# Own rows of a tile gathered four turns ahead instead of five, and the norm of its query three turns ahead instead of four, in a two-layer graph kernel

## The chip, the cores and the metric

The kernel runs on one core of one Trainium2 chip. The metric is device microseconds of one execution. The engines are named as the profile names them: PE is TensorE (PEld its weight loads), DVE is VectorE, ACT is ScalarE, POOL is GpSimd and SP is SyncE. DVE, ACT, PE, POOL and SP each work through a queue of their own in order, and wait for each other with semaphores.

## The reference

There are 4096 nodes with 512 features and an adjacency matrix with few edges: a random one of density 0.000976562, made symmetric, with the diagonal added. Two layers follow each other.

```python
h = jnp.maximum(_layernorm(x), 0.0)
Q, K, V = (h @ W.T for W in (WQ, WK, WV))          # 8 heads of 64
attn = softmax(Q K^T * 0.125 + (Q @ we.T + be), masked by adj)
hard = (attn == max(attn, axis=-1)) / 8            # the best neighbour alone
x = x + hard @ V
h = jnp.maximum(_layernorm(x), 0.0)
agg = (adj > 0) @ h / degree
out = concat(h @ W_self + b_self, agg @ W_nb + b_nb) @ W_comb + b_comb
x = x + relu(out)
```

In the first layer every node takes, for each head, the value row of the one neighbour with the highest score. In the second it takes the mean of its neighbours.

## The kernel before, in words

`sparse_path` does the work (`general_path` follows only for inputs with longer neighbour lists, and did not run). It has three stages.

The first stage (up to about 300 us) normalises all rows, projects keys and values, packs the adjacency matrix into lists of neighbours, sorts the nodes by their number of neighbours, and leaves all of it in a table `K_d` in device memory: a row holds a node's values, keys, list of neighbours with some numbers, and its own x.

The middle stage (about 300 to 905 us) is the one that the change touches. The sorted nodes are cut into 32 tiles of 128 rows. `CAPS` (L512) gives the longest list of each tile, from 24 down to 5. Each tile is worked on in one **turn**; the list `turns` (L1571 to L1573) says which tile comes in which turn, and "place p" below is the tile of turn p. The order is 0, 1, 24, 2, 25, 3, 26, 14, 4, 27, 5, 15, 6, 16, 7, 17 and so on: tiles with long lists ("apart", 0 to 13) and with short ones ("fused", 14 to 31) alternate for most of the stage.

A tile passes through these steps, each written to one or two engines' queues:

- `rows` (L1162): POOL gathers the tile's own rows from `K_d`, by `perm`. They land in one of 8 buffers `km` (1088 numbers a row), or, for the fused tiles of places 15 to 27 ("wide"), in a slot of a large tile `room` (1600 numbers a row). The buffer is read until the addition `xo` (L1318) several turns later, and a new gather into it has to wait for that.
- `query_norm` (L1175): ACT copies the list into `sidx` (L1177) and the row's numbers into `smeta` (L1180), and normalises the row into `hq` (L1182; 2 buffers).
- `query_turn` (L1187): PE transposes `hq` (L1156). `query_copy` (L1190): ACT copies the result into `hqT` (L1193). `query` (L1195): PE projects it into `q` (L636), eight matmuls as the profile counts them.
- `key_gathers` (L1200): POOL gathers the neighbours' rows, one gather of 128 rows for each place in the list. An apart tile's keys go to the 4 buffers `kg`, four neighbours in each. A fused tile's keys and values go together to a region of `room`.
- `scores` (L1238): DVE multiplies with `q` (L1244) and sums by head (L1250), four neighbours at a time.
- `winners` (L1266): DVE finds the best neighbour of each head. A fused tile takes its value at once by predicated copies (L1290) into `o`. An apart tile computes an index (L1312), and POOL gathers the 8 heads' values two or three turns later (`value_gathers`, L1221).
- `own_values` (L1229): POOL gathers a fused tile's own value rows into `o` where they did not come with `rows`.
- `layer1_xo` (L1315): DVE adds x and `o` (L1318). `layer1_stats`, `layer1_norm`, `layer1_turn`, `layer1` and their companions take the tile through the second layer's norm and projections and write it to `G_d` and `X1_d`.

POOL's gathers are all recorded at one line, L1121, in `gather`. The stage is written under a manual schedule: the order of the calls in the loop at L1652 is the order in each engine's queue. The loop runs from -5, so the first tiles' own rows and norms come ahead of turn 0. Within a turn POOL's order is: key gathers, mixed with the value gathers that are due, then `rows`, then `own_values`. ACT's order within a turn has `query_copy`, `layer1_copy`, `layer1_stats`, `query_norm`, `layer1_out`, `layer1_norm` and `ranks` (copies of neighbours' indices, L1264), besides the making of one-hot words (`hot_some`) for the last stage. On PE the product of those words (`hot_product`) comes before the scores of the turn, and `query_turn` at the end of it.

Turn 3 also ends with `fold_bias` (L1471): DVE work on a bias row, with casts (L1478) and subtractions (L1480). Nine value tiles are still projected and written in turns 0 and 1 (L847), and the first fused tile's gathers need them.

In the last stage (905 us to the end) POOL gathers rows of `G_d` for the sums over neighbours, DVE adds them up (L1830), PE does the eight tiles with the longest lists as a dense product (L1805), and the rows go out.

Of the kernel before, what the change touches and what calls it, by code (L numbers as in the profile page):

```python
# [544 lines left out]
def sparse_path(  # L545
# [70 lines left out]
    def load_fold(k):  # L616
        nc.sync.dma_start(
            F[:, ds(2 * k * NC, NC), :],
            (wselfT, wnbT)[k].rearrange("(c p) f -> p c f", p=P),
        )  # L620
        nc.sync.dma_start(
            F[:, ds((2 * k + 1) * NC, NC), :],
            wcomb[ts(k, D), :].rearrange("(c p) f -> p c f", p=P),
        )
# [13 lines left out]
    with ExitStack() as pa:  # L638
# [198 lines left out]
        def values(t, ps):  # L837
            pv = ps.tile([P, D], F32, tag="pm", name="pv")
            project(pv, hT(t), ws["wv"])
            return pv  # L840

        def values_out(t, pv, pool, eng, vs=None):
            if vs is None:
                vs = pool.tile([P, D], F32, tag="gs", name="vs")

            nc.scalar.activation(vs, pv, AF.Copy, scale=1.0 / H)
            return eng.dma_start(K_d[ts(t, P), 0:D], vs)  # L847
# [90 lines left out]
        def on(step, t, *args):  # L938
            if 0 <= t < KT:
                step(t, *args)  # L940
# [170 lines left out]
    with ExitStack() as pb:  # L1111
# [8 lines left out]
        def gather(dst, src, idx, at=0):  # L1120
            last[0] = nc.gpsimd.indirect_dma_start(  # L1121
                out=dst, out_offset=None, in_=src,
                in_offset=bass.IndirectOffsetOnAxis(ap=idx, axis=0), element_offset=at,
            )
            if at:

                beyond.append(last[0])
                for w in written:
                    tc.declare_no_dep(last[0].ins, w.ins, reason="other columns")
# [99 lines left out]
        def own_values(r):  # L1229

            s = st[r]
            if r in wide:
                s["o"] = s["own"][:, 0:D]
            else:
                s["o"] = xp.tile([P, D], F32, tag="o", name="o", bufs=3)
                gather(s["o"], K_d[:, :], perm[:, r : r + 1])
# [22 lines left out]
        def ranks(r, a=None, b=None):  # L1259

            if a is None and r == turns[0]:
                a = 4
            for kk, g0, g in st[r]["kg"][1:][a:b]:
                nc.scalar.copy(sidx[:, ds(sat[r] + g0, g)], kk[:, :, D])  # L1264
# [178 lines left out]
        def load_bias():  # L1443
            for k in range(2):
                fb = bp.tile([P, D], F32, tag=("own", "gs")[k], name="fb", bufs=1)
                for c in range(NC):
                    nc.vector.tensor_copy(
                        fb[:, ts(c, P)], bcs[k][:, c : c + 1].to_broadcast([P, P])
                    )
                fbs.append(fb)  # L1450
# [54 lines left out]
        def hot_some(i):  # L1505

            for _ in range(HOTS // 2):
                if i < FIRST or not hots or pos[hots[0][0]] >= i:
                    break
                if hot_now and hot_now[-1][0] != hots[0][0]:  # L1510
                    break
                r, k = hots.pop(0)
                if k == 0:
                    word_codes(r)
                code = st[r]["code"]
                one = bp.tile([P, SEG], BF16, tag="hot", name="hot", bufs=HOTS)
                nc.scalar.activation(one, ramp, AF.Square, bias=code[:, 0, k : k + 1])  # L1517
                nc.scalar.activation(one, one, AF.Relu, bias=code[:, 1, k : k + 1], scale=-1.0)
                hot_now.append((r, k, one))
# [14 lines left out]
        def words_copy():  # L1534
            for r, k, acc in summed:
                st[r]["wg"] = bp.tile([P, SEG], F32, tag="wst", name="wg", bufs=1)
                nc.scalar.copy(st[r]["wg"], acc)

        def words_turn():

            for r, k, acc in summed:
                if k < CAPS[r] - 2:
                    continue
                pt = pst.tile([P, NC, P], F32, tag="tr", name="tr")
                for h in range(2):
                    nc.tensor.transpose(pt[:, h, :], st[r]["wg"][:, ts(h, P)], ident)
                wi = bp.tile([P, 2, P], I32, tag="wst", name="wi", bufs=1)
                nc.scalar.copy(wi, pt[:, 0:2, :])
                nc.sync.dma_start(W_d[r], wi)
            summed.clear()  # L1550
# [51 lines left out]
        i = 0  # L1602
# [20 lines left out]
        def late(step, kind, i, *args):  # L1623

            out_ = []
            for r in turns:
                if plan[kind].get(r) == i:
                    out_ += step(r, *args) or []
            return out_

        def tail_turn(r):

            k = tail.index(r)
            at = HALF_R + TAIL0 + k * D
            st[r]["hT1"] = room[:, at : at + D].rearrange("p (c q) -> p c q", q=P)
            nc.scalar.copy(st[r]["hT1"], st[r]["hnp"])
# [15 lines left out]
        for i in range(-5, KT):  # L1652


            if i == -3:
                load_fold(0)
            if i == 0:
                load_bias()
                nc.gpsimd.memset(rows3, 0.0)
                for k in range(3):  # L1660
                    nc.gpsimd.memset(rows3[k * Q32 : k * Q32 + 1, :], 1.0)
            if i == KT - 1:
                wT = wp.tile([P, DENSE, SEG + 2], I32, tag="w_a", name="wT")
                nc.sync.dma_start(
                    wT[:, :, 0:SEG], W_d.rearrange("r p h q -> p r (h q)")
                )
            if i == 2:
                wS = wp.tile([P, NC, D], F32, tag="w_b", name="swS")
            if i == 1:
                wN = bp.tile([P, NC, D], F32, tag="swN", name="swN", bufs=1)  # L1670
            a, b = on(key_gathers, i), late(value_gathers, "value", i)
            while a or b:
                for q, n in ((a, max(1, round(len(a) / max(1, len(b))))), (b, 1)):
                    for g in q[:n]:
                        gather(*g)
                    del q[:n]
            on(rows, i + 5)
            if i in (0, 1):
                n = 6 if i == 0 else len(late_v)
                for k, t in enumerate(late_v[:n]):  # L1680
                    vs = xp.tile([P, D], F32, tag="xo", name="vs", bufs=2)
                    w = values_out(t, values(t, psm), None, nc.sync, vs)
                    for g in beyond:
                        tc.declare_no_dep(w.ins, g.ins, reason="other columns")
                    written.append(w)
                    if k < 4 and i == 0:
                        ranks(turns[0], k, k + 1)
                del late_v[:n]
            words_copy()
            late(layer1_move, "move", i)  # L1690
            on(query_copy, i + 2)
            late(layer1_copy, "layer1", i)
            early = [r for r in tail if plan["turn"][r] == i - 1]
            for r in early:
                tail_turn(r)
            if i >= 0 and turns[i] in fused:
                own_values(turns[i])
            on(query, i + 1)
            late(layer1_close, "move", i)
            words_turn()  # L1700
            hot_some(i)
            late(layer1_stats, "stats", i)
            on(query_norm, i + 4)
            late(layer1_out, "move", i)
            hot_some(i)
            for part in between.get(i, ()):
                fold(*part)
            late(layer1, "layer1", i)
            for r in early[: -1 if i == KT - 1 else None]:
                tail_product(r)  # L1710
            hot_product()

            def within():
                late(layer1_inverse, "stats", i)

            if i >= 0:
                scores(turns[i], within)
            if i == KT - 2:
                gsl = [gp.tile([P, GRP, D], F32, tag="kg", name="gs") for _ in range(2)]
            on(winners, i)  # L1720
            late(layer1_norm, "stats", i)
            if i == max(between):
                fold_bias()
            on(ranks, i)
            on(query_turn, i + 3)
            if i < KT - 1:
                late(layer1_turn, "turn", i)
                for r in early:
                    tail_move(r)
# [209 lines left out]
```

## Time and profile before

| | |
|---|---|
| median of 3 runs (lowest to highest) | 1190.85 us (1189.97 to 1191.04) |
| the profiled execution's own time | 1188.29 us |
| its span, first to last instruction | 1186.5 us |
| mean granted TensorE clock | 0.928 |
| moved by DMAs | 348.44 MB, mean 294 GB/s |
| own-rows gathers into `km` (L1121) | 25, of 0.94 us on POOL; 4.4, 5.5 and 9.8 us (least, median, most) to landing |
| norms of a query (L1182) | 32, of 0.81 us on ACT |

The page gives for each engine its busy time, its share of the span and its instructions. A group's line has the source line, the engine, the operation, the tile written and those read. In the views of waits, "A <- B" means that A stood idle and that B ended the wait. In the view by time a bracket holds the idle time before an instruction and what ended it; "issue" is time in which nothing that the profile shows was waited for. A view of windows gives each engine's busy time between two moments. All moments are microseconds from the start of the span.

### The profile page before, as it was taken

How to read it: one execution, taken by the hardware profiler on the slowest of the kernel's cores; microseconds unless marked ns; L12 is line 12 of the kernel's file. 1: busy time of each engine (PE TensorE's matmuls, PEld its weight loads, DVE VectorE, ACT ScalarE, POOL GpSimd, SP SyncE). 2: the span in 40 equal slices, each digit the busy share in tenths (PEclk: the TensorE clock that was granted, in tenths of full speed). 3: DMA queues.
4: the chain of work that ended last, by engine and by line, in shares of the span. 5: the costliest groups of instructions: out<-in, count | busy, mean ns of one | idle time of the engine just before them, and what ended most of it. 6: DMA issues, size and time to landing. Idle time of an engine off the chain costs nothing. (4 is left out here: it accounts for less than half of the span.)

```text
span 1186.5 us, 11454 instructions
## 1 busy us (share of the span) xinstructions
PE 1023.9 (86%) x3079; PEld 501.6 (42%) x3079; DVE 982.7 (83%) x1548; ACT 550.1 (46%) x1222; POOL 715.1 (60%) x939
## 2 busy tenths in 40 slices
PE   3999999979599668688879989888989999999792
PEld 1555555644244224344334434444434444444340
DVE  4358789889289798798989999999983699998894
ACT  3777777932222377486567678754462100000000
POOL 3332323312677757757777777777713777777774
PEclk9999999989799878889889889888999999999996
DMA  9999999979797678889898889988865888888973
GB/s 353 418 420 418 413 418 375 396 226 293 229 269 251 180 233 261 255 278 292 281 289 281 284 280 298 291 279 280 284 256 171 306 310 275 321 288 276 369 242 108
DMA packets 115594, 348.44 MB, mean 294 GB/s; under 512 B 21472, under 2 KB 23552, under 8 KB 107328
## 3 DMA queue, kind: packets, MB, share of 16 engines
q0 software_dynamic: 60560, 201.01, 53.0%
q1 hardware_dynamic: 50560, 146.56, 32.5%
q10 hardware_dynamic: 4400, 0.05, 0.3%
q8 instruction: 26, 0.43, 0.1%
q14 instruction: 48, 0.39, 0.1%
HBM read 287.75 MB, written 64.00 MB: 296 GB/s over the span
## 5 line engine op out<-in xcount | busy, mean ns | idle before, releaser
L1805 PE MATMUL da<-gk,mk 128*128 128x512 f32 x512 | 223.2, 599 | 6.9 <-DVE mk L1556 6.2
L1121 POOL DMA_INDIRECT room<-G_d,sidx x174 | 168.5, 969 | 84.6 <-issue 80.7
L636 PE MATMUL q<-wq,hqT 128*128 128x512 f32 x256 | 151.0, 745 | 51.3 <-DVE pr L1244 51.3
L1250 DVE TENSOR_REDUCE sc<-pr 128x32 f32<-128x2048 f32 (+3 forms) x114 | 183.3, 1608 | 3.8
L1121 POOL DMA_INDIRECT kg<-K_d,sidx x161 | 153.4, 953 | 49.0 <-issue 40.2
L1830 DVE TENSOR_REDUCE acc<-room 128x512 f32<-128x4096 f32 (+5 forms) x23 | 153.0, 6651 | 32.5 <-DMA room<-G_d,sidx 30.6
L1805 PEld LDWEIGHTS da<-gk,mk 128*128 128x128 f32 x512 | 98.2, 192 | 131.9 <-issue 123.1
L1121 POOL DMA_INDIRECT room<-K_d,sidx x118 | 111.6, 945 | 42.9 <-issue 25.6
L1121 POOL DMA_INDIRECT o<-K_d,vi x112 | 108.1, 965 | 34.2 <-issue 32.0
L636 PE MATMUL pk<-wk,room 128*128 128x512 f32 x256 | 118.5, 606 | 2.6 <-ACT room L821 2.6
L636 PE MATMUL pv<-wv,room 128*128 128x512 f32 x256 | 112.6, 592 | 0.0
L636 PEld LDWEIGHTS q<-wq,hqT 128*128 128x128 f32 x256 | 59.2, 243 | 123.0 <-issue 77.7
L1244 DVE TENSOR_TENSOR pr<-q,kg 128x2048 f32<-128x2048 f32 (+3 forms) x47 | 93.3, 1985 | 11.2 <-DMA kg<-K_d,sidx 10.1
L1393 PE MATMUL pr<-swS,hT 128*128 128x512 f32 x216 | 97.1, 592 | 0.0
L636 PE MATMUL pg<-swN,hT 128*128 128x512 f32 x216 | 97.1, 593 | 0.0
L760 ACT ACTIVATE mkt<-adjt,sgb 128x2048 bf16<-128x2048 int32 x44 | 88.0, 1999 | 2.1 <-POOL adjt L678 2.1
L1244 DVE TENSOR_TENSOR pr<-q,room 128x2048 f32<-128x2048 f32 (+3 forms) x42 | 73.2, 1744 | 18.1 <-DMA room<-K_d,sidx 16.0
L636 PEld LDWEIGHTS pv<-wv,room 128*128 128x128 f32 x256 | 48.3, 190 | 59.3 <-issue 59.1
L636 PEld LDWEIGHTS pk<-wk,room 128*128 128x128 f32 x256 | 47.5, 196 | 51.5 <-issue 47.8
L830 DVE SCALAR_TENSOR_TENSOR ks<-pk,swe 128x512 f32<-128x512 f32 x32 | 21.9, 686 | 52.5 <-PE pk L636 46.8
L1517 ACT ACTIVATE hot<-ramp,code 128x256 bf16<-128x256 bf16 x105 | 52.5, 500 | 22.5 <-DVE code L1498 22.5
L779 PE MATMUL pw<-mkt,planes 128*128 128x256 bf16 x512 | 62.8, 277 | 0.0
(254 smaller groups left out, 1619.5 us busy)
## 6 DMA issues: line engine op xcount, KB each, us to landing
adjt<-adj_dram SPq DMA_DIRECT2D x44, 1024.0 KB, 10.4
room<-adj_dram SPq DMA_DIRECT2D x20, 1024.0 KB, 11.0
x<-X_d SPq DMA_DIRECT2D x25, 512.0 KB, 7.8
xt<-x_dram SPq DMA_DIRECT2D x32, 256.0 KB, 8.1
K_d<-ks POOLq DMA_DIRECT2D x32, 256.0 KB, 6.5
X_d<-xo SPq DMA_DIRECT2D x32, 256.0 KB, 4.5
G_d<-gs SPq DMA_DIRECT2D x32, 256.0 KB, 3.9
gk<-G_d SPq DMA_DIRECT2D x16, 512.0 KB, 4.8
```

Source lines behind the costliest of these rows:

```text
L636: nc.tensor.matmul(dst, h[:, c, :], w[:, c, :], start=(c == 0), stop=(c == NC - 1))
L760: nc.scalar.activation(mk, st[t]["adj"][j], AF.Sigmoid, bias=sgb, scale=400.0, accum_out=degs[:, t, j : j + 1],)
L779: nc.tensor.matmul(pw, planes[:, s, :], st[t]["mk"][j][:, ts(i, SEG)], start=False, stop=(s == NPL - 1),)
L830: nc.vector.scalar_tensor_tensor(ks.rearrange("p (h d) -> p h d", h=H), st[t]["pk"].rearrange("p (h d) -> p h d", h=H), HD**-0.5, web.unsq ...
L1121: last[0] = nc.gpsimd.indirect_dma_start(out=dst, out_offset=None, in_=src, in_offset=bass.IndirectOffsetOnAxis(ap=idx, axis=0), element_o ...
L1244: nc.vector.tensor_tensor(pr[:, :g, :], s["q"].unsqueeze(1).to_broadcast([P, g, D]), kk[:, :, 0:D], ALU.mult)
L1250: nc.vector.tensor_reduce(sc[:, g0 : g0 + g, :], pr[:, :g, :].rearrange("p g (h d) -> p g h d", h=H), AX.X, ALU.add,)
L1393: nc.tensor.matmul(pr, s["hT1"][:, c, :], wS[:, c, :], start=False, stop=(c == NC - 1 and mine is None and not open_))
L1517: nc.scalar.activation(one, ramp, AF.Square, bias=code[:, 0, k : k + 1])
L1805: nc.tensor.matmul(dacc[r], masks[s][:, r, h, :], keys[s][:, h, :], start=(s == 0 and h == 0), stop=(s == NPL - 1 and h == 1),)
L1830: nc.vector.tensor_reduce(acc, g[:, 0:n, :].rearrange("p n f -> p f n"), AX.X, ALU.add)
```

## The change

The own rows of a tile are asked for four turns before its own turn, not five, and the norm of its query is asked for three turns before, not four. The transposes, the copy and the projection of the query keep their turns (three, two and one before).

```diff
@@ -1674,7 +1674,7 @@
                     for g in q[:n]:
                         gather(*g)
                     del q[:n]
-            on(rows, i + 5)
+            on(rows, i + 4)
             if i in (0, 1):
                 n = 6 if i == 0 else len(late_v)
...
@@ -1700,7 +1700,7 @@
             words_turn()
             hot_some(i)
             late(layer1_stats, "stats", i)
-            on(query_norm, i + 4)
+            on(query_norm, i + 3)
             late(layer1_out, "move", i)
             hot_some(i)
```

`on(step, i)` calls a step for the tile of place i where there is one. In both kernels one turn lies between a tile's `rows` and its `query_norm`.

## The prediction

> **What bounds the kernel now.** I read the page first, then a table of windows over the middle stage (312 to 905 us, where both edits lie), then what DVE and POOL waited for in it, and last the two engines in order of time around the longest waits. The page's first part, for the whole span:
>
> ```profile
> PE 1023.9 (86%) x3079; PEld 501.6 (42%) x3079; DVE 982.7 (83%) x1548; ACT 550.1 (46%) x1222; POOL 715.1 (60%) x939
> ```
>
> POOL's 60% misleads, as the windows show (columns: length; busy time and instructions of PE, weight loads, DVE, ACT, POOL; clock; DMA share; GB/s):
>
> ```profile
> 312.00:416.50 104.50, 93.32 (x227) 42.68 (x228) 83.34 (x78) 27.85 (x73) 79.19 (x86) 0.91 0.80 240
> 416.50:423.30 6.80, 1.10 (x4) 0.30 (x3) 6.39 (x16) 1.24 (x3) 0.03 (x1) 0.91 0.57 227
> 423.30:507.90 84.60, 63.56 (x178) 31.19 (x177) 72.72 (x85) 58.75 (x155) 64.44 (x67) 0.82 0.83 254
> 507.90:516.00 8.10, 5.93 (x13) 2.95 (x12) 7.79 (x13) 6.47 (x18) 0.00 (x0) 0.50 0.77 307
> 516.00:700.00 184.00, 154.71 (x427) 74.21 (x426) 170.44 (x208) 127.00 (x338) 139.47 (x147) 0.88 0.89 283
> 700.00:860.00 160.00, 144.97 (x406) 69.02 (x405) 153.42 (x197) 99.66 (x273) 121.29 (x128) 0.94 0.90 284
> ```
>
> From 516 to 700, 147 gathers in 184.0 us are 1.25 us each; 700 to 860 gives 160/128 = 1.25 again. A gather is busy 0.94 us and followed by 0.30 us of issue: POOL issues without a break, though it counts as 76% busy. Only the second and fourth rows hold nothing on POOL. DVE is 93 to 96% busy from 516 on. So two engines run neck and neck: DVE computes, POOL feeds it. What DVE, then POOL, waited for from 312 to 905 (total us, times, longest):
>
> ```profile
> DVE pr L1244 <- DMA room<-K_d,sidx: 16.0, 7, 5.1
> DVE pr L1244 <- DMA kg<-K_d,sidx: 10.1, 5, 3.3
> DVE o L1290 <- DMA o<-K_d,perm: 2.2, 1, 2.2
> ```
> ```profile
> POOL km L1121 <- DVE xo L1318: 14.9, 2, 8.1
> POOL room L1121 <- ACT sidx L1264: 7.2, 1, 7.2
> ```
>
> DVE waits for gathers that come late; POOL itself was held twice, by an own-rows gather waiting for a buffer. POOL in order of time (start, us, instruction, idle before and releaser), at each hold:
>
> ```profile
> 415.59 0.93 POOL L1121 DMA_INDIRECT room<-K_d,sidx  x1 [0.31 <-issue]
> 423.32 0.94 POOL L1121 DMA_INDIRECT km<-K_d,perm  x1 [6.80 <-DVE xo L1318]
> ...
> ```
> ```profile
> 506.94 0.94 POOL L1121 DMA_INDIRECT room<-K_d,sidx  x1 [0.30 <-issue]
> 516.02 0.94 POOL L1121 DMA_INDIRECT km<-K_d,perm  x1 [8.14 <-DVE xo L1318]
> ```
>
> DVE a turn and a half after the first hold:
>
> ```profile
> 466.98 4.58 DVE L1290 COPY_PREDICATED o<-best,room 128x512 f32<-128x512 int32 x6 [2.16 <-DMA o<-K_d,perm]
> ...
> 476.06 2.29 DVE L1244 TENSOR_TENSOR pr<-q,room 128x2048 f32<-128x2048 f32 x1 [2.60 <-DMA room<-K_d,sidx]
> ...
> 485.82 2.29 DVE L1244 TENSOR_TENSOR pr<-q,room 128x2048 f32<-128x2048 f32 x1 [5.09 <-DMA room<-K_d,sidx]
> ```
>
> These three waits (9.85 us) follow the first hold. After the second DVE waits 3.10 (turn 11, at 557.0), 3.31 (turn 13), 0.51 (15), 1.36 (17; the view blames its own reciprocal, but the gather landed at 667.29 and DVE went on at 667.37), 1.06 (27) and 0.35: 9.69 us.
>
> **The change, part by part.** No instruction is added or dropped: 32 own-rows gathers, 32 norms (three ACT instructions each), the same DMAs. SP's order is the same; PE's is the same but for names; DVE moves one small `half`. POOL's and ACT's orders move.
>
> *The two holds.* In the old order turn 4 asks for place 9 (tile 27), which takes the km buffer that the addition at 422.36 to 423.05, in turn 4 itself, frees. In the new one turn 4 asks for place 8, whose buffer the addition ending at 390.4 freed; place 9 comes in turn 5, behind 12 key gathers, long after 423. Turn 9 asked for place 14 and waited for the addition ending at 515.75, of turn 9; now it asks for place 13 and waits for that of turn 8, at 499.0, some 7 us before POOL wants it, while the wait on 515.75 moves behind turn 10's gathers. POOL thus gains 6.80 - 0.30 = 6.50 us and 8.14 - 0.30 = 7.84 us.
>
> *One gather less ahead.* Four own-rows gathers, not five, stand before the first key gather, so key gathers come one slot (1.25 us) earlier. Part is lost. ACT now copies the first turned query before the second norm: the copy waits for PE until 313.0, so the second norm ends near 314.75 instead of 313.66, and place 0's query starts about 1.0 us later. Its matmuls run 0.855 us apart until 318.9 and 0.43 us after, so 1.04/0.855 = 1.2 matmuls move into the fast part: 0.5 us later at the end. DVE's first product (320.80) has room: it then waits 4.2 us for gathers in turn 0. But the value writes behind it land at 360.56, and place 2's first gather needs them; the new order wants that gather at 360.60, 1.24 us sooner than 361.84. With writes 0.5 us later I keep 0.5 of the 1.25 (ends: -0.9, were PE slow for one more 3.4 us, to 1.25).
>
> PE's clock row gives 0.5 until 318.9 and 1.0 after it; throughout the trace it changes on a 3.41 us grid. The Trainium skill (TensorE: Matmul & The Clock Gate, What's actually happening) has a free-running window of 3413 ns, one busy window of which releases the clock. By that rule the release stays at 318.9, as the query fills the window before it; were two busy windows needed, the query would end 1.9 us later and the 0.5 kept would be -0.9.
>
> *POOL beside the bias fold.* In the first hold DVE runs the fold: six casts of 0.42 us, three subtractions of 0.68 us (L1478 and L1480, 416.5 to 421.9). Five gathers will now stand beside them; the trace shows none there. Nearest rows: gathers that start within DVE's xo addition take 1.30, 1.37 and 1.36 us (437.08, 454.92, 471.58) instead of 0.94. Ends: 0, and 4.5 us if POOL stops for all nine. I take three subtractions times 0.4 = 1.2 us.
>
> The Trainium skill (SBUF — State Buffer, Who interferes with whom) says that a DVE copy or cast in a two-port mode shuts GpSimd out for the whole instruction. By it the casts cost too, up to the 4.5 us; the sum would be 3.3 us less. No run here shows it yet.
>
> *The sum.* POOL's lead S is 0.5 up to turn 4, 0.5 + 6.5 - 1.2 = 5.8 from turn 5, and 5.8 + 7.84 = 13.6 from turn 10. DVE's gain G rises only where it waited for a gather, and never above S. Turn 3: 0.5. Turn 7: min(0.5 + 9.85, 5.8) = 5.8. Turn 11: 8.9; 13: 12.2; 15: 12.7; 17: min(14.1, 13.6) = 13.6. It stays there. From 867 the chain is DVE's (POOL waits 7.2 us for ACT's copies and then 31.9 us for the last G_d write), so the last stage moves as a whole.
>
> *Is POOL stopped elsewhere?* Other waits on DVE in its queue leave enough: gathers into a fused tile's region need the predicated copies of the fused tile two turns before, with 7.1 us to spare in turn 13, 4.9 in 15, 4.5 in 17, 2.4 in 21. POOL's growth over DVE (S less G) is then 4.7, 1.4, 0.9 and 0. Buffers of keys leave some 10 us or more.
>
> *The norm.* PE's transposes of place i+3 stand at the end of turn i; the norm now stands in that turn, at the slot where place i+4's stood. That slot ended 1.1 us before PE came in turn 0 and at least 3.0 us before in all later turns, so I cost it at nothing; without that cover PE would wait, but the query it holds up is needed a turn later. The four own rows asked one turn later still land a turn before their norm.
>
> Profiled execution: 1188.29 us (span 1186.5) less 13.6 = 1174.7. It lies 2.56 us under the median 1190.85, from which the forecast is **1177.2 us**.
>
> **The rivals.**
> *DMA takes it back.* From 516 the 16 engines are 0.89 to 0.90 busy. From 416.5 to 516.0 they did 6.8 x 0.57 + 84.6 x 0.83 + 8.1 x 0.77 = 80.3 us of work; at 0.89 this needs 90.2 instead of 99.5 us, 9.3 saved of 14.3. With the 0.5 and without the fold's 1.2 that is a gain of 9.8, 1181; were the engines full at 0.85 already, 80.3 / 0.85 = 94.5 us would leave 5.5, 1185. For it: that share. Against: POOL's cadence held at 0.90.
> *The fold takes 4.5 us,* POOL standing still beside all nine instructions: S ends 3.3 us lower, gain 10.3, 1180.5. For it: the stretched gathers beside an addition. Against: they were stretched by 0.4 us, not by the addition's 0.68.
> *Slower, by landings.* A gather waits for the landing of the eighth before it. Eight slots are 10 us; the longest landing is 9.8 us (issue 341.61), medians near 5.5. Were landings to pass 10 us, each us over costs 0.125 us a gather: at 12 us over the 340 gathers from 423 on, 85 us; over 100 of them 25, net +11: 1202. It decides from 10 us. Against: holds only empty the DMAs, and without them the cadence is that of 516 to 860.
> *The hold only moves* to another buffer: 1190.8, plus or minus 1. Against: the additions and slots above.
>
> **How the numbers follow.** Forecast 0.64 (1172 to 1180), DMA takes part back 0.12 (1181 to 1185), the fold takes its 4.5 us 0.07 (1180.5), nothing 0.05, slower 0.12. The low end is the full 1.25 + 14.34 = 15.6, 1.2 of spread in the runs and up to 1.7 of PE clock in the tail (it ran at half for 3.4 us at 879). Range 1172 to 1184.5. A measurement of this kernel can tell about 0.2%, 2.4 us: faster 0.83, same 0.05, slower 0.12.
>
> **What would show it.** Right: POOL's row for km waiting on xo gone; gathers 1.25 us apart from 312 past 860; DVE's three waits at turns 6 and 7 down to one of some 4 us, and none over 1 us from turn 11 to 17; the stage's end near 891 instead of 905. Wrong: transposes waiting on hq past turn 0; gathers over 1.3 us apart with longer landings; POOL idle before another gather.

## The result, and the profile after

The changed kernel takes 1173.6 us (median of 4 runs, 1170.91 to 1175.15) against 1190.41 us for the kernel before beside it (4 runs, 1188.65 to 1191.04): a ratio of 0.9859, 95% interval 0.9837 to 0.9881. The forecast was 1177.2 us, range 1172 to 1184.5. The profiled execution took 1170.91 us, with a span of 1169.2 us.

The page's first part, which hardly differs from before, since no work went:

```profile
PE 1019.3 (87%) x3079; PEld 499.6 (43%) x3079; DVE 982.4 (84%) x1548; ACT 549.2 (47%) x1222; POOL 715.1 (61%) x939
```

The windows of the middle stage at the same moments as before (length; busy time and instructions of PE, weight loads, DVE, ACT, POOL; clock; DMA share; GB/s):

```profile
416.50:423.30 6.80, 0.74 (x2) 0.21 (x2) 6.44 (x15) 2.78 (x7) 5.28 (x6) 0.76 0.95 336
423.30:507.90 84.60, 67.41 (x186) 33.27 (x186) 78.70 (x94) 63.19 (x168) 63.87 (x69) 0.82 0.88 280
507.90:516.00 8.10, 8.10 (x20) 3.54 (x19) 7.96 (x8) 7.47 (x21) 6.27 (x7) 0.94 0.97 316
516.00:700.00 184.00, 158.52 (x458) 77.17 (x457) 177.63 (x225) 127.93 (x340) 139.50 (x147) 0.91 0.90 288
```

In the two stretches in which POOL did next to nothing it now issues 6 and 7 gathers, and between them DVE is busy for 78.70 of 84.60 us where it was for 72.72. From 516 to 700 POOL again issues 147 gathers, and DVE is 97% busy. What DVE waited for from 312 to 890 us, and the own-rows gather of turn 9 in POOL's order of time:

```profile
DVE pr L1244 <- PE q L636: 19.0, 1, 19.0
DVE pr L1244 <- DMA kg<-K_d,sidx: 9.0, 4, 3.2
DVE pr L1244 <- DMA km<-K_d,perm: 3.6, 1, 3.6
DVE q L1348 <- ACT q L1334: 1.6, 2, 1.1
DVE pr L1244 <- DMA room<-K_d,sidx: 1.1, 1, 1.1
```
```profile
498.90 0.93 POOL L1121 DMA_INDIRECT km<-K_d,perm  x1 [0.30 <-issue]
500.14 0.95 POOL L1121 DMA_INDIRECT o<-K_d,perm  x1 [0.31 <-issue]
501.39 0.95 POOL L1121 DMA_INDIRECT kg<-K_d,sidx  x1 [0.30 <-issue]
```

POOL's row for `km` held by the addition is gone, and with it DVE's 16.0 us for gathers into `room`; 1.1 us of those are left, beside one wait of 3.6 us in turn 7. (That one is named after `km`, though the product that waits reads keys in `room`.)

To see where the time left, I count from the first own-rows gather (305.68 us before, 304.01 after, as the first stage, which the change doesn't touch, ran 1.67 us shorter here). The moment of the maximum in `winners`, turn by turn:

| turn | 3 | 6 | 7 | 9 | 11 | 13 | 15 | 17 | 31 | first gather of `G_d` |
|---|---|---|---|---|---|---|---|---|---|---|
| before, us | 107.6 | 158.6 | 185.1 | 218.8 | 256.2 | 294.7 | 330.4 | 366.6 | 582.9 | 599.76 |
| after, us | 107.4 | 158.6 | 179.0 | 212.9 | 247.9 | 283.0 | 317.9 | 352.7 | 567.8 | 585.00 |
| earlier by | 0.2 | 0.0 | 6.1 | 5.9 | 8.3 | 11.7 | 12.5 | 13.9 | 15.1 | 14.8 |

The two profiled executions differ by 17.38 us: 1.67 in the first stage, 14.76 in the middle one, 0.8 in the last (281.0 against 280.2 us), and some 0.1 outside the span. Only the 14.76 can be laid to the change: in the first four experiments below, whose first stage is the same too, the first own-rows gather stands anywhere from 304.5 to 305.9 us and the last stage lasts 279.8 to 281.1 us. 14.76 us lies in the interval of the ratio (14.2 to 19.4 us).

### The profile page after: what moved, and what is told of

The parts are those of the page before. It is cut to its first block, busy times and chain, and to the rows that moved or that the text cites. A ratio compares the mean times of both kernels' runs of the same rounds, so it can differ in the third digit from the quotient of the medians.

```text
span 1169.2 us, 11470 instructions
## 1 busy us (share of the span) xinstructions
PE 1019.3 (87%) x3079; PEld 499.6 (43%) x3079; DVE 982.4 (84%) x1548; ACT 549.2 (47%) x1222; POOL 715.1 (61%) x939
## 4 chain that ended last, share of the span: by engine, by line
PE 31%; DVE 24%; DMA 19%; POOL 12%; issue 9%; ACT 4%; POOLq 0%; DVEq 0%; ACTq 0%; SPq 0%
PE pk L636 7%; POOL room L1121 7%; DVE pr L1244 6%; PE pv L636 6%; DMA room<-G_d,sidx 5%; DVE sc L1250 4%; PE q L636 4%; PE pw L779 4%; DMA room<-K_d,sidx 3%; DVE acc L1830 3%; PE pr L1393 3%; PE pg L636 3%; PE pmw L636 2%; DMA kg<-K_d,sidx 2%; DMA km<-K_d,perm 2%
## 5 line engine op out<-in xcount | busy, mean ns | idle before, releaser
L636 PE MATMUL q<-wq,hqT 128*128 128x512 f32 x256 | 147.9, 732 | 42.8 <-DVE pr L1244 42.8
```

What stands on the lines that cost most here:

```text
L636: nc.tensor.matmul(dst, h[:, c, :], w[:, c, :], start=(c == 0), stop=(c == NC - 1))
```

## The experiments

In the first four runs the kernel before took 1188.3 us (median of 19 runs) and the changed kernel was not run beside them; its gain of 16.8 us on the medians would put it at 1171.5 us there.

### The order alone: seven buffers in the changed kernel

```diff
-                km = xp.tile([P, ROWX], F32, tag="km", name="km", bufs=8)
+                km = xp.tile([P, ROWX], F32, tag="km", name="km", bufs=7)
```

> The changed kernel with seven km buffers instead of eight: its order is kept, but place 8's rows now wait for the addition of turn 4 and place 13's for that of turn 9, as places 9 and 14 did in the kernel before. Theory (holds): POOL stands again for 6 to 8 us near 421 and 514 us, and the time is that of the kernel before, 1190 us (1188.5 to 1191.5). Rival (order): it keeps the changed kernel's time, 1173.6 plus or minus 1.5.

1188.34 us, ratio 0.9994 (0.998 to 1.0008). Both holds are back, in POOL's order of time:

```profile
422.40 0.94 POOL L1121 DMA_INDIRECT km<-K_d,perm  x1 [6.62 <-DVE xo L1318]
...
515.27 0.94 POOL L1121 DMA_INDIRECT km<-K_d,perm  x1 [8.34 <-DVE xo L1318]
```

With the changed kernel's order of instructions on every engine, but POOL held as before, the whole gain is gone. It came from the holds, and the order by itself is worth nothing.

### The norm alone

```diff
-            on(query_norm, i + 4)
+            on(query_norm, i + 3)
```

> Only the second half of the change: rows still asked five turns ahead, the norm three turns ahead. Theory (holds): both holds stay, and the later second norm costs up to 0.5 us at the start: 1190.5 us (1189 to 1191.5). Rival (the norm's place on ACT brings the gain): 1173 to 1180.

1189.16 us, ratio 1.0007 (0.9997 to 1.0018). POOL waits for the addition as before, 6.70 us at 423.15 and 8.35 us at 515.68. Moving the norm brings nothing.

### The rows alone

```diff
-            on(rows, i + 5)
+            on(rows, i + 4)
```

> Only the first half: rows asked four turns ahead, the norm left four turns ahead, so that ACT waits in the same turn for the rows just asked. From the changed kernel's trace the norm's slot stands before that landing by 2 us in turn 0, 8 in turn 1, 10 in turn 2, 18 in turn 3, 8 in turn 7, and about 1 or nothing else. Theory (holds): the holds go, ACT's waits cost something only where its later copies are needed at once: 1177 us (1174 to 1182). If ACT's waits all reach DVE, as much as the holds gave is lost again and the time is 1190 or more. Rival (the norm's place brings the gain): 1190.

1175.39 us, ratio 0.9886 (0.9858 to 0.9914): 12.9 of the 16.8 us. POOL's holds are gone. What ACT waited for from 312 to 905 us:

```profile
ACT sidx L1177 <- DMA km<-K_d,perm: 80.0, 12, 18.9
ACT sidx L1177 <- DMA room<-K_d,perm: 30.7, 6, 6.6
ACT hn L1332 <- DVE xo L1318: 25.9, 14, 5.1
```

ACT stands for 111 us in 18 waits for rows that have just been asked for, up to 18.9 us at a time, and these cost little: turn 3 ends 1.4 us later than in the changed kernel (108.75 against 107.36 us after the first gather), and turns 7 to 17 within 0.2 us of it. From there to turn 31 2.6 us are lost (570.4 against 567.8), and 4.0 us up to the first gather of `G_d`. The losses of the turns come as DVE's waits for gathers, in turns 25, 27 and 28 above all. POOL's gathers of wide rows stand 1.3 us later than in the changed kernel from the first of them on (place 15) and up to 2.3 us later in the end, but from turn 7 on that costs DVE time in those late turns alone. ACT works for later turns here. The second half of the change is worth these few us at most, and only together with the first.

### A spare buffer instead of another order

```diff
+            elif r == turns[9]:
+                km = big[:, KT * D - ROWX : KT * D]
+                gather(km, K_d[:, :], perm[:, r : r + 1], D)
             else:
                 km = xp.tile([P, ROWX], F32, tag="km", name="km", bufs=8)
```

(three lines more, so DVE's L1290 is L1293 here.)

> The kernel before, with one buffer more: place 9's own rows land in a free stretch of the key buffer, so nothing has to be freed for them, and place 14 takes the buffer freed in turn 8. Asked five turns ahead and normed four ahead, as before. Theory (the two holds of POOL are the whole cost): both holds vanish and 6.2 + 7.8 = 14.0 us go, 1176.4 us against 1190.4 before, with nothing of the prologue's slot. Rival (the gain comes from the order itself, key gathers a slot earlier and norms closer to their use, and the holds are covered anyway): 1190, plus or minus 1.

1180.29 us, ratio 0.9929 (0.9906 to 0.9952): 8 us on the medians, not 14. Both waits for a buffer are gone, as meant: place 9's rows are asked at 415.47 without a pause. But POOL stands again in turn 10, and DVE at that time:

```profile
514.75 0.94 POOL L1121 DMA_INDIRECT kg<-K_d,sidx  x1 [0.30 <-issue]
523.34 0.94 POOL L1121 DMA_INDIRECT room<-K_d,perm  x1 [7.65 <-ACT hot L1521]
```
```profile
520.31 2.29 DVE L1293 COPY_PREDICATED o<-best,room 128x512 f32<-128x512 int32 x3
522.49 0.68 DVE L1321 TENSOR_TENSOR xo<-km,o 128x512 f32<-128x512 f32 x1
```

This is the own-rows gather of place 15, the first of the wide ones. Its slot is columns 13000 to 14600 of `room` (slot 3: 8200 + 3 x 1600), and place 9's six neighbours lie in columns 8192 to 14342. So it waits for the last predicated copy of turn 9, which ends at 522.60 (the ACT instruction in the bracket is only the one that ended nearest to the start; the last semaphore that POOL waits for ahead of this gather is DVE's, at 522.64). In the kernel before this wait was there too, behind the second hold: the gather came at 532.70, when the copy had ended at 529.76. Take the second hold away and a third, of 7.65 us, stands a turn later. The changed kernel asks for place 15 in turn 11, at 536.75, 14.6 us after the copy (522.15).

So my expectation failed, for a wait that no view of the kernel before lists. Up to there the run confirms the first hold's price: at turn 9 the maximum stands at 212.9 us after the first gather, 5.9 earlier than before, as in the changed kernel. From there the gain only goes to 8.5 us in turn 17, where the changed kernel has 13.9; that kernel differs here in having the third wait gone as well. The gain does not last either: in turns 25 and 27 DVE waits 1.43 and 1.83 us for gathers, 6.5 us are left at turn 31 and 5.0 at the first gather of `G_d`. What makes POOL later there isn't shown. The profiled execution is 7.1 us shorter than the one before, and 1.9 of these lie in the first and last stage.

### Parts of the change by place

The rest were to price each hold by itself. In all of these the kernel before itself took 1466 to 1477 us (medians), on several chips, one of them that of the first four runs; what made it so isn't known.

Places 9 to 13 alone:

```diff
-            on(rows, i + 5)
+            if 9 <= i + 4 <= 13:
+                on(rows, i + 4)
+            if not 9 <= i + 5 <= 13:
+                on(rows, i + 5)
```

(and the norm in the same way)

> The kernel before, with the change for places 9 to 13 alone (rows four ahead, norm three ahead); all other places as before, so place 14 is still asked in turn 9 and must wait for the addition of turn 9. Theory (each hold has its own worth, POOL's lead adds up): only the first hold goes, POOL gains 6.2 us from 423 us on, DVE has them by turn 7, the hold near 510 us stays as long as it was (about 8 us): 6.0 us less than the kernel before (5 to 7). Rival (what the first gives, the second takes: DVE's addition is no earlier and POOL only waits longer for it): 0 to 1 us less, with a second hold of some 14 us.

1455.79 us against 1467.45, ratio 0.9898 (0.9858 to 0.9937). The place-14 kernel's first run and the place-9 kernel, which follow, were run beside it.

All places from 14 on:

```diff
-            on(rows, i + 5)
+            if i + 5 < 14:
+                on(rows, i + 5)
+            elif i + 4 >= 14:
+                on(rows, i + 4)
```

(and the norm in the same way)

> The kernel before, with the change from place 14 on alone: places 0 to 13 as before, so the first hold stays and the second goes; place 15's wide rows are asked in turn 11 and not behind turn 9's last predicated copy, which held them in the run with the spare buffer. Theory: the first hold stays at 6.8 us, POOL gains 7.8 us from 508 us on, DVE's waits in turns 11 to 17 (8.3 us together) pay them out: 7.8 us less than the kernel before (6.5 to 8.5). Rival (the DMA engines, 0.89 busy from 516 us on, have no room for it): 3 us less or nothing.

1457.26 us, ratio 0.9925 (0.9905 to 0.9945); then twice more, 1460.83 and 1471.42 us, with ratios of 0.9989 (0.9949 to 1.003) and 0.9999 (0.9973 to 1.0024):

> The same kernel once more, on a chip that runs the kernel before near 1190 us: the change from place 14 on alone. Theory: the first hold stays at some 6.8 us, POOL gains 7.8 us from 508 us on, DVE's waits in turns 11 to 17 (8.3 us together) pay them out: 7.8 us less than the kernel before (6.5 to 8.5), a ratio of 0.9934. Rival (the DMA engines, 0.89 busy from 516 us on, have no room for it): 3 us less or nothing, 0.9975 or more.

> The change from place 14 on alone, a third time, in the hope of a chip that runs the kernel before near 1190 us. Theory: the first hold stays at some 6.8 us, POOL gains 7.8 us from 508 us on, DVE's waits in turns 11 to 17 (8.3 us together) pay them out: 7.8 us less than the kernel before (6.5 to 8.5), a ratio of 0.9934. Rival (the DMA engines, 0.89 busy from 516 us on, have no room for it): 3 us less or nothing, 0.9975 or more.

All places from 9 on (the same edit with 9 for 14):

> The kernel before, with the change from place 9 on: both holds go, but five own-row gathers stand before the first key gather, as before, and ACT's order at the start is the old one. It leaves out of the change only the slot at the start. Theory (the slot is lost at the value writes in turn 2, the holds are all): within 0.5 us of the changed kernel, some 16.5 us less than the kernel before on the medians; DVE's first wait for a key gather in turn 0 about as long. Rival (the slot is worth its full 1.25 us): 15.5 us less.

1453.14 us, ratio 0.9891 (0.9862 to 0.9919). DVE's, then ACT's longest waits in its middle stage (312 to 1104 us):

```profile
DVE q L1348 <- ACT q L1334: 196.9, 13, 21.9
```
```profile
ACT hqT L1193 <- remote: 97.5, 11, 27.7
ACT wg L1537 <- remote: 96.1, 6, 24.0
ACT swS L1464 <- remote: 36.4, 2, 36.2
```

Here DVE waits for ACT, and ACT for something that the trace doesn't name (all three copies take what PE has made), and POOL, whose gathers still take 0.94 us, itself stands 7 to 18 us in about every second turn for what these two do. The holds that were left have other lengths too: the first is 17.57 us in the first run from place 14 on (6.8 was expected), the second 21.15 us with places 9 to 13 (8 was expected). POOL's supply is not what bounds this, so the price of a hold can't be read from it, and the expectations of these runs can't be judged. One thing can. Turn 9's maximum stands 266.6 and 271.8 us after the first gather where the first hold is gone (places 9 to 13, places 9 on) and 292.9 to 295.7 us where it stays (three runs of places 14 on); by turn 17 it is 491.2 and 484.0 against 481.8 to 491.4 us. So over 20 us lie between the two kinds at turn 9, and 8 turns later nothing certain is left of them. What each hold is worth by itself near 1190 us stays untested for the second; the first is priced above.

### Two tries to go further

The changed kernel with the norm of place 1 ahead of the first copy again:

```diff
-            on(query_norm, i + 3)
+            if i != -2:
+                on(query_norm, i + 3)
+            if i == -3:
+                on(query_norm, 1)
```

> The changed kernel, with the norm of place 1 put back ahead of the first copy of a turned query, as in the kernel before. Theory (that order cost the changed kernel 0.4 us up to the value writes, which hold POOL at turn 2): the first product and the writes come 0.4 us earlier, POOL's wait of 0.7 us at 360 us shrinks to 0.3, and the time is 0.3 us under the changed kernel's, 17 us less than the kernel before; too small to be told by the time, to be read in the trace. Rival (the writes wait for something else): the wait at 360 us stays.

1446.54 us, ratio 0.986 (0.9829 to 0.9891), run beside places 9 to 13. Up to 320 us these runs are like all others, so the start can be compared: the first product comes 14.72 us after the first own-rows gather, against 15.50 in the changed kernel. Over all profiled executions (without the rows alone) it is 14.5 to 15.1 us in the eight with the second norm ahead of the copy, 14.7 on the mean, and 15.2 to 15.7 us in the five with it behind, 15.5 on the mean. So that order does cost some 0.75 us at the start on the means, and 0.4 between the kernel before and the changed one; I had put it at 0.5. What it is worth at the value writes can't be read, as POOL's wait there is 8.8 us in this run, as PE's products come late.

The value gathers of two places a turn later:

```diff
                 v = p + 3 if p + 2 > FIRST and turns[p + 2] in apart else p + 2
+                v += p in (1, 5)
```

> The changed kernel, with the eight value gathers of place 1 moved from turn 3 to turn 4 and those of place 5 from turn 7 to turn 8; the additions that need them stay in turns 5 and 9. It asks what DVE's last waits of any size (2.6 and 3.2 us in turn 3, 3.6 us in turn 7) are worth. Theory (POOL issues without a break up to turn 17 and DVE's gain never exceeds POOL's lead): the waits go from turns 3 and 7 and come back behind the moved gathers, in turns 4 to 17, some 9 us in all; the time stays that of the changed kernel within 1.5 us, 0.986 of the kernel before. Rival (a wait taken away is time gained): 5 to 9 us less than the changed kernel, 0.979 to 0.982 of the kernel before.

> The same kernel once more, for a chip that runs the kernel before near 1190 us: the changed kernel with the value gathers of place 1 moved from turn 3 to turn 4 and those of place 5 from turn 7 to turn 8. Theory (POOL issues without a break up to turn 17 and DVE's gain never exceeds POOL's lead): DVE's waits go from turns 3 and 7 and come back in turns 4 to 17; 0.986 of the kernel before within 0.0015. Rival (a wait taken away is time gained): 0.979 to 0.982 of the kernel before.

1456.11 and 1473.2 us, ratios 0.9945 (0.9913 to 0.9978) and 0.9968 (0.9937 to 1.0). Neither the 0.986 of the theory nor the rival's 0.979 to 0.982 came out, and as above POOL's supply can't be priced under these conditions; whether DVE's last waits are worth anything near 1190 us stays open.

## Why the prediction was right, point by point

**The two holds: right, and shown.** Put back by seven buffers, they take the whole gain; with the norm alone moved they stay, and so does the time. The last key gather of turn 4 and the first of turn 5 stood 10.23 us apart (415.59, 425.82) and now 3.80 (413.76, 417.56): 6.43 us, against 6.50 less the fold's share. POOL's lead at the first key gather of turn 10, counted from the first own-rows gather, is 15.46 us (212.84 against 197.38) where I had 13.6; three terms of the sum make the difference:

- **One gather less ahead** was put at 0.5 us and gave about 0.16 (that last key gather of turn 4 stands 109.91 and 109.75 us after the first own-rows gather). It was lost at the value writes, as I said: the last of them landed 55.20 us after the first own-rows gather against 54.88, and POOL, whose last wait ends with it, asks for place 2's first neighbour at 56.01, against 56.16 before. The reason that I gave, the second norm behind the copy, fits the start of the first product in all runs (above). The clock was no part of it: its row goes from 0.5 to 1.0 at 317.7 us, 13.7 us after the first own-rows gather, and before at 319.6, 13.9 after it. (The prediction's 318.9 is where the last slow matmul starts, 0.7 us too early; its 0.5 us doesn't hang on that.)
- **The fold** was put at 1.2 us and cost POOL 0.25: of the gathers beside it, three in a row, and DVE beside them,

```profile
416.24 1.01 POOL L1121 DMA_INDIRECT o<-K_d,perm  x1 [0.31 <-issue]
417.56 1.12 POOL L1121 DMA_INDIRECT kg<-K_d,sidx  x1 [0.30 <-issue]
418.98 0.95 POOL L1121 DMA_INDIRECT kg<-K_d,sidx  x1 [0.30 <-issue]
```
```profile
416.20 0.92 DVE L1478 CAST same<-sbb 32x512 bf16<-32x512 f32 x2
417.16 0.68 DVE L1480 TENSOR_TENSOR sbb<-sbb,same 32x512 f32<-32x512 f32 x1
...
419.50 0.54 DVE L1481 COPY sbb<-same 96x512 bf16<-96x512 bf16 x1
```

  only two took more than 0.95 us. The first stood beside two casts (416.20 to 417.13) and lost 0.07 us. The second started 0.29 us before the end of a subtraction and lost 0.18; no other started within a subtraction with more than 0.03 us of it left, and I had charged 0.4 us for each of the three. The rival with 4.5 us is refuted. In this row the Trainium skill's rule (SBUF — State Buffer, Who interferes with whom) that a cast in a two-port mode, where it comes first, shuts GpSimd out for the whole instruction is not seen: the gather started 0.04 us after the first cast, and both became 0.07 us longer. But five other runs agree with it. In each a gather that started 0.05 us after such a cast, with 0.37 us of it left, took 1.19 us, so it waited for most of the cast. (Two more, in the second run of the later value gathers, started 0.04 us after one and lost nothing; there the cast took 0.08 us more.) With places 9 on:

```profile
449.81 0.42 DVE L1478 CAST same<-sbb 32x512 bf16<-32x512 f32 x1
449.85 1.19 POOL L1121 DMA_INDIRECT kg<-K_d,sidx  x1 [0.30 <-issue]
```

  What the rival had wrong is that POOL waits beside every instruction of the fold; it waits only where a gather starts within one, and for the rest of that one. (Whether the casts ran in a two-port mode the trace doesn't tell.) A part of the price fell on DVE, which the sum left out: its copy L1481 took 0.54 us with a gather under way since 418.98 (0.53 in the runs with the rows alone and with the spare buffer), and 0.29 in the kernel before, where no gather ran beside it.
- **A term that I didn't have:** 1.2 us. From the first key gather of turn 5 to that of turn 9 POOL's lead grows from 6.59 to 7.62 us with no hold between; the second hold then adds its 7.84 to the hundredth. Before, three gathers there started within an addition (437.08, 454.92, 471.58) and took 1.30 to 1.37 us, 1.2 more than usual; after, none does, and the 0.18 of the fold's second gather, which falls here, leaves 1.0. I had used these rows for the fold's price and not seen that they would go.

**DVE's gain by turns: right in size, turn 17 for another reason.** Forecast 5.8, 8.9, 12.2, 12.7, 13.6 for turns 7, 11, 13, 15, 17; measured 6.1, 8.3, 11.7, 12.5, 13.9. In turn 7 POOL's lead is the limit, as I said, and 3.6 us of DVE's waits are left. In turn 17 I had the lead (13.6) as the limit; in truth it was larger, and DVE had run out of waits: 6.1 and the 8.3 us of turns 11 to 17 make 14.4, less a new one of 0.5 us at 546.76. The lead's error of 1.8 us thus hardly shows up to there. After turn 17 the waits at 829 us and later give another 1.2 us, up to 15.1 at turn 31; the sum had let the gain stay at 13.6, its lead.

**DMA takes it back: refuted.** From 423.3 to 507.9 the share rose to 0.88 and to 0.97 in the stretch behind it, from 516 to 700 it is 0.90 against 0.89, and POOL's cadence is 147 gathers in 184 us both times. Median landing after 516 us is 5.24 us against 5.14, and the longest of all is 9.4 us, so **the slower case**, landings over 10 us, did not come near.

**The hold moves: refuted for this change, but it was closer than I knew.** I weighed the buffers and the gathers into `room` of fused tiles, and not the slots of wide places, whose first gather would have been held for 7.65 us had it kept its turn. The change moves that gather too, so nothing came of it. That was luck, and not the forecast's working.

**The norm costs nothing: right.** From 312 us on PE waits for `hq` once, 1.7 us at 313.06, and where ACT was made to wait 111 us, the loss in the middle stage was 4.0 us.

**The total.** 13.6 us was forecast, all of it in the middle stage, and 14.8 is measured there in the profiled executions. The other 2 us of the 16.8 on the medians lie in stages with the same instructions and are not explained by any step; the profiled executions, where the first and last stage gave 2.5, suggest chance, but no run settles it.

## What to carry to other kernels

A queue that is 60% busy over the span may issue without a break; look at the distance between its instructions, and treat each stop as lost only up to what its consumer later waits for. When an instruction held for a buffer is moved or given a buffer, list what the instructions behind it on the queue wait for as well, since a wait that ends just before them today becomes the next hold: moving the whole class by one turn cleared three at once, one buffer cleared two and met the third. To learn whether an order or a hold made a gain, keep the new order and bring the hold back, by one buffer less.

## What the runs showed of the hardware that was not expected

A gather issued by POOL is stretched if it starts within DVE's addition `xo`, and by what is left of it. Of ten that did from 312 to 865 us in the changed kernel, six had 0.49 to 0.60 us of it left and took 1.31 to 1.42 us; two with 0.28 and 0.17 us left took 1.10 and 0.98. All eight take 0.94 us and what is left of the addition, less 0.12 us, to within 0.02 us. The other two started within 0.005 us of the addition's own start and took 0.94, and the 21 that had started before the addition took 0.93 to 0.95 throughout. The first engine in keeps its pace, and the second waits for it to end; so the 0.4 us that the prediction read as the price of an addition was only the rest of it. The gathers beside a cast of the fold that took 1.19 us fit the same sum (0.94 + 0.37 - 0.12). The Trainium skill (SBUF — State Buffer, Who interferes with whom) says that a DVE instruction with two inputs in SBUF contends with a GpSimd instruction that reads SBUF, and that the order of issue decides who waits; both fit this addition.

The kernel before took 1188.3 us on one chip and, later, 1477.3 us on the same chip (medians). In the later runs the first 305 us are as ever; after that there are long gaps between PE's products and ACT's copies of them. In the kernel changed from place 9 on, PE's last product of a group ends at 395.7 us by the profile, the semaphore of PE that ACT's copy waits for is updated at 422.75, and the copy starts at 422.77. No instruction of PE lies between:

```profile
422.77 0.58 ACT L1464 COPY swS<-pmw 128x512 f32<-128x512 f32 x1 [36.17 <-remote]
```

What delays them stays open.
